# A four-layer graph network on one NeuronCore: 512 of the 2048 columns of an attention step on GpSimd

## The chip, the cores and the metric

The kernel runs on one core of a Trainium2 chip. A core has five engines that run side by side, each through its own queue and in order: TensorE (PE) multiplies matrices into PSUM, VectorE (DVE) and ScalarE (ACT) work element by element and can read PSUM, GpSimd (POOL) works element by element on SBUF, and SyncE (SP) issues the loads. Semaphores order the engines among themselves. The metric is the device time of one execution in microseconds (us), smaller is better. A measurement of this kernel tells a difference of about 0.5%, some 5 us.

## The reference

x has 4096 rows of 64 columns, adj is a 4096 x 4096 matrix of zeros and ones. Four layers follow one another, each x = layernorm(x + layer(x, adj)): a mean over neighbours with a linear map (layer 0), hyperbolic attention (1), a weighted sum in which the weights halve from neighbour to neighbour (2), and hyperbolic attention again (3). The change is in the attention, which layers 1 and 3 share:

```python
x_t = logmap0(x, c)
left = x_t @ w_att[:D, 0]
right = x_t @ w_att[D:, 0]
adj_att = jax.nn.sigmoid(left[:, None] + right[None, :] + b_att[0]) * adj
x_local = logmap(x[:, None, :], x[None, :, :], c)
support_t = jnp.einsum('ij,ijd->id', adj_att, x_local)
return proj(expmap(x, support_t, c), c)
```

For each pair of nodes (i, j) there is one weight: the sigmoid, the edge, and a factor out of logmap (an artanh of the distance over the distance). The sum over j of weight times x_j is a matrix product. So the 16.8 million weights of a layer are the elementwise work, and the rest is small work on rows.

## The kernel before

The 4096 target nodes are cut into four groups of WW = 1024 (GROUPS = 3, 2, 1, 0) and the 4096 source nodes into 32 blocks of 128 (also from the last to the first). attend (L1064) handles one group of one layer. It runs over g = 15 to 0; each g is a pair of blocks, k = 1 and then k = 0, so a layer has 4 x 16 = 64 pairs. In the texts below the pairs of a layer are counted in the order in which they run, from 0 to 63.

For each block of a pair:

- TensorE computes z (128 sources x 1024 targets) in two halves of 512 columns, each from three matmuls: the edges times a constant (L1098), and two products of row data (L1101, L1104). Where there is no edge z is negative.
- ScalarE computes sig, the sigmoid of left plus right (L1113), and sq, the square of a linear function of z (L1116).
- VectorE computes t = max(z, 0) x sig (L1119), with z from PSUM.

After both blocks VectorE does the second pass over the pair, 2048 columns at once: t = (sq + HIGH²) x t (L1121). The product of the two passes is the factor of logmap times the sigmoid. TensorE then adds up t times the source rows xe, in float32, into one PSUM bank for the group (add_up, L1071 to L1082): first k = 1, both halves, then k = 0. This is delayed by two pairs: the list lag holds (g, t), and add_up of a pair is written behind the z products of a later pair.

Buffers: z has three PSUM tiles, sq two tiles of a pair, t three, sig three. So TensorE can be up to three z tiles ahead, and sq of pair g + 2 goes where sq of pair g stood.

The order on TensorE and ScalarE is laid down by the order in which the kernel's text issues work and by dependencies (manual_schedule, FIXED); VectorE's and GpSimd's queues are ordered by the scheduler when the program is built. Between the pairs lies the row work. It is written as generators that tick (L616) advances: every pair ticks at least three times, and each generator says in how many ticks it wants to go on. Three of them matter here:

- norm_rows (L894) and prepare (L914): normalize the rows of a group of nodes and make from them what the next layer's attention needs (hi_lo, lo_hi, src, dst, xe, left, right). Attention can only handle a source block when prepare is done for its group (need, L1086), so the first 16 pairs of a layer run beside this.
- move (L1137): takes the sums of a finished group through expmap, projection and layernorm to the next x. For all groups but the last of a layer it runs on GpSimd (class Small, on_pool), as some ninety operations on 128 x 8 numbers and four on 128 x 512 (L1184, L1265, L1266, L1269), beside the pairs of the following group. VectorE and ScalarE take a part in it: two reductions (L1187, L1189), the first step of each reciprocal square root (L762, three times), a reciprocal (L1233) and a tanh (L1215). Each of these is in the queue of its engine between the operations of the pairs and waits there for GpSimd, and GpSimd waits for it in turn.
- the last group's move runs on VectorE (and in layer 3 it is the end of the kernel).

All loads of adj go through SP's queue, in tiles of 1 MB with six buffers.

Of the kernel before, what the change touches and what calls it, by code (L numbers as in the profile page):

```python
# [15 lines left out]
ALU = mybir.AluOpType  # L16
# [7 lines left out]
W = 512  # L24
# [5 lines left out]
WW = 1024  # L30
# [15 lines left out]
HIGH = 1.3261200051291  # L46
# [14 lines left out]
def gnn_stack_kernel(  # L61
# [15 lines left out]
    nc = tc.nc  # L77
    V = nc.vector
# [492 lines left out]
    def stream(fits):  # L571

        with ExitStack() as st:
# [42 lines left out]
            def tick(n):  # L616
                for _ in range(n):
                    place[1] += 1
                    mark(False)
                    for queue in queues:  # L620
                        while queue and queue[0][1] <= place[1]:
                            wait = next(queue[0][0], None)
                            if wait is None:
                                queue.pop(0)
                                continue
                            queue[0][1] = place[1] + wait
                            if wait:
                                break
                    mark(True)

            def later(steps, second=False, wait=0):
                queues[int(second)].append([steps, place[1] + wait])

            def in_turn(tag, *parts):
                for part in parts:
                    yield from (part or ())
                done.add(tag)
# [5 lines left out]
            def need(tag):  # L643
                while tag not in done:
                    assert any(queues), tag
                    tick(1)
# [53 lines left out]
            def load(s, g):  # L700
                a = loads.tile([P, 2, WW], F32, name="edges")
                nc.sync.dma_start(a, adj[s, :, 2 * g : 2 * g + 2, :])

                return a, a.rearrange("p b i -> p (b i)").bitcast(BF16)[:, 1::2]
# [9 lines left out]
            def nums(name, n=WB):  # L714
                return row.tile([P, n], F32, name=name)
# [320 lines left out]
            def in_order(one, behind):  # L1036

                tc.add_manual_dep(
                    one, behind.name,
                    mybir.DependencyInfo(  # L1040
                        mybir.DependencyClass.NoSync, mybir.DependencyReason.DATA
                    ),
                    reason="order of issue",
                )

            def spread_left(s):

                left_bs[s] = lefts.tile([P, WW], F32, name="left_b")
                for h in range(2):
                    yield from free()  # L1050
                    t = take(F32, P, W)
                    for k in range(SB):
                        nb = s * WB + h * SB + k
                        nc.tensor.transpose(
                            t[:, k * P : (k + 1) * P],
                            left[:, nb : nb + 1].to_broadcast([P, P]),
                            ident,
                        )
                    yield near()
                    nc.scalar.copy(left_bs[s][:, h * W : (h + 1) * W], t)  # L1060
                    held.pop()
                    yield 1

            def attend(layer, s, rate, then):  # L1064

                left_b = left_bs[s]

                acc = ps.tile([P, W], F32, name="acc")
                lag = []

                def add_up(g, t, behind=None):  # L1071

                    for k in (1, 0):
                        j = 2 * g + k
                        for h in range(2):
                            it = nc.tensor.matmul(  # L1076
                                acc[h * D : (h + 1) * D, :], xe[:, j, :],
                                t[:, k, h * W : (h + 1) * W],
                                start=j == BLOCKS[0], stop=j == BLOCKS[-1],
                            )  # L1080
                            if behind is not None:
                                in_order(it.ins, behind.ins)  # L1082

                for g in reversed(range(NB // 2)):
                    _, edge = load(s, g)
                    need((layer, 2 * g // WB))  # L1086
                    if g == 4 and then is not None:
                        later(in_turn((layer, then, "left"), spread_left(then)), True)
                    for k in (1, 0):
                        j = 2 * g + k  # L1090
                        of = slice(j * P, (j + 1) * P)

                        zp = z_tile()
                        for h in range(2):
                            half = zp[:, h * W : (h + 1) * W]
                            to = slice(s * WW + h * W, s * WW + (h + 1) * W)
                            at = k * WW + h * W
                            nc.tensor.matmul(  # L1098
                                half, two_i, edge[:, at : at + W], start=True, stop=False
                            )  # L1100
                            nc.tensor.matmul(  # L1101
                                half, hi_lo[:, of], lo_hi[:, to], start=False, stop=False
                            )
                            last = nc.tensor.matmul(  # L1104
                                half, src[:, of], dst[:, to], start=False, stop=True
                            )
                        if k == 1:
                            if len(lag) == 2:
                                add_up(*lag.pop(0), last)
                            sq = sb.tile([P, 2, WW], F32, name="sq")  # L1110
                            t = sb.tile([P, 2, WW], F32, name="t", bufs=3)
                        sig = sb.tile([P, WW], F32, name="sig", bufs=3)
                        nc.scalar.activation(  # L1113
                            sig, left_b, AF.Sigmoid, bias=right[:, j : j + 1]
                        )
                        nc.scalar.activation(  # L1116
                            sq[:, k], zp, AF.Square, bias=ROOT + OFF, scale=-1.0 / UNIT
                        )
                        V.scalar_tensor_tensor(t[:, k], zp, 0.0, sig, ALU.max, ALU.mult)  # L1119
                        tick(rate)  # L1120
                    V.scalar_tensor_tensor(t, sq, HIGH**2, t, ALU.add, ALU.mult)  # L1121
                    lag.append((g, t))
                    tick(rate)
                for args in lag:
                    add_up(*args)
                sums = row.tile([P, W], F32, name="sums", bufs=2)
                nc.scalar.copy(sums, acc)
                return sums
# [377 lines left out]
            def z_tile():  # L1506
                return ps.tile([P, WW], F32, name="z", bufs=3)

            def attention(layer, curve, rates, behind):

                need((layer, GROUPS[0]))
                for n, s in enumerate(GROUPS):
                    if n:
                        need((layer, s, "left"))
                    anchored[0] = n > 0
                    then = GROUPS[n + 1] if n + 1 < NW else None
                    sums = attend(layer, s, rates[n], then)
                    move_s = in_turn((layer, s, "moved"), move(layer, s, sums, curve))
                    if n:
                        later(  # L1520
                            in_turn((layer + 1, s + 1), there((layer, s + 1, "moved")), behind(s + 1)),
                            True, 9,
                        )
                    apart = 2 if n + 1 == NW and layer == 1 else 0
                    later(move_s, apart)
                    if n + 1 == NW:
                        later(in_turn((layer + 1, s), behind(s)), apart)
                anchored[0] = False
# [174 lines left out]
            t, g = nums("m1", 1), nums("g1", 1)  # L1703
# [4 lines left out]
            sq = row.tile([P, D], F32, name="w_sq")  # L1708
# [21 lines left out]
    with tc.tile_pool(name="fit_ps", bufs=1, space=PSUM) as ps:  # L1730
        t = ps.tile([1, P], F32, name="fit_t")
# [52 lines left out]
```

## Time and profile before

| | |
|---|---|
| three runs | 1073.8, 1074.14, 1077.64 us (median 1074.14) |
| the profiled execution | 1073.46 us |
| its span, first to last instruction | 1071.7 us |
| attention of layer 1, first to last L1121 | 198 to 516 us |
| attention of layer 3, first to last L1121 | 728 to 1039 us |

The span is what the trace shows; the execution has 1.8 us around it. A row of the page's groups reads: line, engine, operation, out<-in with partitions x elements, count, then the busy time of the group in us, the mean duration of one in ns, and the engine's idle time just ahead of it with what ended that. The chain of waits is followed back from the last instruction; its shares say which engine's work lay on the way to the end. Spans on GpSimd include the time in which an operation has started and can't reach its data. The two rows of GpSimd's largest groups in attention, and the row of the tensor engine's accumulation:

```profile
L1076 PE MATMUL acc<-t,xe 128*64 128x512 f32 x1024 | 260.0, 614 | 10.6 <-DVE t L1121 9.7
...
L901 POOL TENSOR_TENSOR sq<-z 128x512 f32<-128x512 f32 x8 | 16.2, 2024 | 168.4 <-DVE z L900 147.3
L1184 POOL TENSOR_TENSOR w_att<-x,u 128x512 f32<-128x512 f32 x6 | 12.7, 2122 | 139.7 <-ACT u L1179 139.7
```

The means of 2024 and 2122 ns hold short and long ones: single operations of this size take from 1.04 to 3.03 us in the trace.

### The profile page before, as it was taken

What the parts mean: (1) busy time and instruction counts of PE and PEld (TensorE: products, weight loads), DVE (VectorE), ACT (ScalarE), POOL (GpSimd) and SP (SyncE); (2) the same over time, 40 slices, a digit from 0 to 9 for tenths busy, and PEclk for the clock granted to TensorE, in tenths of its full rate; (3) what the DMA queues carried; (4) which work ended last, traced back from release to release, by engine and by line L of the source; (5) the groups of instructions that cost most, each with busy time, mean ns of one, the idle gap of its engine ahead of it and who ended that gap; (6) DMA issues with size and microseconds to landing.
All of it is one profiled execution on the core that took longest, in us unless ns stands there. A gap on an engine that the chain in (4) does not pass through costs nothing.

```text
span 1071.7 us, 13656 instructions
## 1 busy us (share of the span) xinstructions
PE 985.7 (92%) x4845; PEld 401.4 (37%) x4845; DVE 919.6 (86%) x1501; ACT 754.4 (70%) x877; POOL 272.3 (25%) x649
## 2 busy tenths in 40 slices
PE   4997998789999999999999989998899999999980
PEld 2454554333333333333333334443333333333320
DVE  7676888999999999999485698829999999999976
ACT  0013122879988889888677778898898888898850
POOL 0011211010044515425500021101102444444162
PEclk9999999989999999999999999999999999999985
DMA  9999999645666656657699979896465666666300
GB/s 340 387 424 356 381 416 377 256 167 197 235 205 227 229 202 210 227 192 240 226 358 324 385 282 342 292 327 223 148 237 194 245 221 209 239 230 229 135 1 24
DMA packets 38580, 271.62 MB, mean 253 GB/s; under 512 B 4710, under 2 KB 4710, under 8 KB 5734
## 3 DMA queue, kind: packets, MB, share of 16 engines
q1 hardware_dynamic: 37728, 270.03, 69.2%
q8 instruction: 40, 0.66, 0.2%
q10 hardware_dynamic: 774, 0.63, 0.2%
q14 instruction: 38, 0.31, 0.1%
HBM read 269.58 MB, written 1.05 MB: 253 GB/s over the span
## 4 chain that ended last, share of the span: by engine, by line
PE 61%; DVE 25%; ACT 6%; DMA 3%; POOL 2%; issue 2%; ACTq 0%; SPq 0%; POOLq 0%; DVEq 0%
PE acc L1076 17%; PE z L1641 9%; PE z L1098 8%; PE z L1104 7%; PE z L1101 7%; DVE t L1119 6%; DVE t L1121 6%; PE acc L1465 4%; DVE junk L844 3%; DMA edges<-in_adj_dram 2%; ACT sq L1648 2%; PE acc L1653 2%; ACT sq L1116 1%; PE z L1653 1%; ACT sig L1113 1%
## 5 line engine op out<-in xcount | busy, mean ns | idle before, releaser
L1119 DVE SCALAR_TENSOR_TENSOR t<-z,sig 128x1024 f32<-128x1024 f32 x256 | 309.8, 1219 | 12.8 <-ACT sq L1116 10.9
L1121 DVE SCALAR_TENSOR_TENSOR t<-sq,t 128x2048 f32<-128x2048 f32 x128 | 295.2, 2307 | 0.2
L1116 ACT ACTIVATE sq<-z 128x1024 f32<-128x1024 f32 x256 | 254.2, 1021 | 56.6 <-PE z L1104 21.6
L1113 ACT ACTIVATE sig<-left_b,right 128x1024 f32<-128x1024 f32 x256 | 286.9, 1149 | 5.3 <-DVE t L1119 4.5
L1076 PE MATMUL acc<-t,xe 128*64 128x512 f32 x1024 | 260.0, 614 | 10.6 <-DVE t L1121 9.7
L1098 PE MATMUL z<-edges,two_i 128*128 128x512 bf16 x512 | 200.9, 392 | 5.5 <-DVE t L1119 5.4
L1104 PE MATMUL z<-dst,src 74*128 74x512 f16 x512 | 194.7, 380 | 0.0
L1101 PE MATMUL z<-lo_hi,hi_lo 128*128 128x512 f16 x512 | 193.8, 378 | 0.0
L1648 ACT ACTIVATE sq<-z 128x512 bf16<-128x512 f32 (+1 forms) x192 | 137.8, 741 | 45.3 <-PE z L1641 44.7
L1076 PEld LDWEIGHTS acc<-t,xe 128*64 128x64 f32 x1024 | 64.3, 137 | 140.5 <-issue 106.0
L1465 PE MATMUL acc<-edges,first 128*128 128x512 bf16 x256 | 80.8, 397 | 17.4 <-DMA edges<-in_adj_dram 17.2
L1098 PEld LDWEIGHTS <-two_i 128*128 128x128 bf16 x512 | 50.3, 98 | 120.5 <-issue 74.5
L1641 PE MATMUL z<-edges,pass_by 128*128 128x512 bf16 x248 | 87.2, 391 | 4.9 <-ACT sq L1648 4.6
L844 DVE SCALAR_TENSOR_TENSOR t<-edges 128x2048 bf16<-128x2048 f32 x32 | 73.0, 2287 | 21.4 <-DMA edges<-in_adj_dram 21.0
L1641 PE MATMUL z<-edges,enter 128*128 128x512 bf16 x256 | 88.8, 389 | 0.0
L844 DVE SCALAR_TENSOR_TENSOR junk<-edges 128x2048 bf16<-128x2048 f32 x32 | 73.1, 2284 | 9.0 <-DMA edges<-in_adj_dram 8.8
L1465 PE MATMUL acc<-edges,third 128*65 128x512 bf16 x256 | 80.4, 396 | 0.0
L1104 PEld LDWEIGHTS <-src 74*128 74x128 f16 x512 | 49.2, 96 | 72.1 <-issue 9.2
L1101 PEld LDWEIGHTS <-hi_lo 128*128 128x128 f16 x512 | 50.2, 98 | 60.6 <-issue 14.6
L901 POOL TENSOR_TENSOR sq<-z 128x512 f32<-128x512 f32 x8 | 16.2, 2024 | 168.4 <-DVE z L900 147.3
L1184 POOL TENSOR_TENSOR w_att<-x,u 128x512 f32<-128x512 f32 x6 | 12.7, 2122 | 139.7 <-ACT u L1179 139.7
L1465 PEld LDWEIGHTS <-first 128*128 128x128 bf16 x256 | 24.3, 98 | 45.1 <-issue 16.2
(402 smaller groups left out, 987.3 us busy)
## 6 DMA issues: line engine op xcount, KB each, us to landing
edges<-in_adj_dram SPq DMA_DIRECT2D x256, 1024.0 KB, 4.9
x<-in_x_dram SPq DMA_DIRECT2D x4, 256.0 KB
out_dram<-x ACTq DMA_DIRECT2D x2, 256.0 KB
out_dram<-x SPq DMA_DIRECT2D x2, 256.0 KB
w_sb<-in_L_gnn_W_dram ACTq DMA_DIRECT2D x1, 32.0 KB, 4.7
w_twice<-in_L_gnn_weight_dram ACTq DMA_DIRECT2D x2, 16.0 KB, 8.7
given<-in_L_gnn_b_dram ACTq DMA_DIRECT2D x1, 0.2 KB
given<-in_L_gnn_bias_dram ACTq DMA_DIRECT2D x1, 0.2 KB
```

The source lines that it names most:

```text
L844: V.scalar_tensor_tensor(junk, a, 0.0, a, ALU.not_equal, ALU.not_equal, accum_out=odd[:, n : n + 1])
L1076: it = nc.tensor.matmul(acc[h * D : (h + 1) * D, :], xe[:, j, :], t[:, k, h * W : (h + 1) * W], start=j == BLOCKS[0], stop=j == BLOCKS[-1],)
L1098: nc.tensor.matmul(half, two_i, edge[:, at : at + W], start=True, stop=False)
L1101: nc.tensor.matmul(half, hi_lo[:, of], lo_hi[:, to], start=False, stop=False)
L1104: last = nc.tensor.matmul(half, src[:, of], dst[:, to], start=False, stop=True)
L1113: nc.scalar.activation(sig, left_b, AF.Sigmoid, bias=right[:, j : j + 1])
L1116: nc.scalar.activation(sq[:, k], zp, AF.Square, bias=ROOT + OFF, scale=-1.0 / UNIT)
L1119: V.scalar_tensor_tensor(t[:, k], zp, 0.0, sig, ALU.max, ALU.mult)
L1121: V.scalar_tensor_tensor(t, sq, HIGH**2, t, ALU.add, ALU.mult)
L1465: nc.tensor.matmul(accs[h][:m], lhs[:, j, :], edge[:, at : at + W], start=j == BLOCKS[0], stop=j == BLOCKS[-1],)
L1641: nc.tensor.matmul(z[:, h : h + W], lhs, rhs[:, h : h + W], start=j == BLOCKS[0], stop=True, skip_group_check=True,)
L1648: weighed[0] = nc.scalar.activation(w, z[:, :n], AF.Exp, bias=-(OFF_EDGE + CUT) * LN2, scale=-LN2)
```

## The change

The second pass over a pair is split. t and sq are seen as flat rows of 2048 columns. VectorE handles columns 0 to 1535 (all of k = 0 and the first half of k = 1) as before. The last 512 columns (the second half of k = 1) go to GpSimd, [...]it does an addition in place in sq and then a product into t.

```diff
@@ -1118,7 +1118,16 @@
                         )
                         V.scalar_tensor_tensor(t[:, k], zp, 0.0, sig, ALU.max, ALU.mult)
                         tick(rate)
-                    V.scalar_tensor_tensor(t, sq, HIGH**2, t, ALU.add, ALU.mult)
+                    flat_sq, flat_t = (o.rearrange("p k i -> p (k i)") for o in (sq, t))
+                    mine, its = slice(0, 2 * WW - W), slice(2 * WW - W, 2 * WW)
+                    V.scalar_tensor_tensor(
+                        flat_t[:, mine], flat_sq[:, mine], HIGH**2, flat_t[:, mine],
+                        ALU.add, ALU.mult,
+                    )
+                    nc.gpsimd.tensor_scalar(
+                        flat_sq[:, its], flat_sq[:, its], HIGH**2, None, ALU.add
+                    )
+                    nc.gpsimd.tensor_mul(flat_t[:, its], flat_t[:, its], flat_sq[:, its])
                     lag.append((g, t))
                     tick(rate)
                 for args in lag:
```

Everything else is the same text. As VectorE's and GpSimd's queues are ordered when the program is built, the neighbours of these operations in the queues can differ from before.

## The prediction

> **What bounds the kernel now.** First the page's table of engines and its chain of waits, then the groups, then the timeline of a quiet stretch. One *pair* g means two source blocks (k=1, then k=0); a layer has 64 pairs, and m(g) and S(g) below are the VectorE steps L1119 and L1121 of pair g.
>
> ```profile
> span 1071.7 us, 13656 instructions
> PE   985.7 (92%) x4845; PEld 401.4 (37%) x4845; DVE 919.6 (86%) x1501; ACT 754.4 (70%) x877; POOL 272.3 (25%) x649
> ...
> PE 61%; DVE 25%; ACT 6%; DMA 3%; POOL 2%; issue 2%; ACTq 0%; SPq 0%; POOLq 0%; DVEq 0%
> ...
> L1119 DVE SCALAR_TENSOR_TENSOR t<-z,sig 128x1024 f32<-128x1024 f32 x256 | 309.8, 1219 | 12.8 <-ACT sq L1116 10.9
> L1121 DVE SCALAR_TENSOR_TENSOR t<-sq,t 128x2048 f32<-128x2048 f32 x128 | 295.2, 2307 | 0.2
> ```
>
> The page makes TensorE the bound and VectorE the second. That is an average; what the change is worth is read in attention. A row of the timeline is start, duration, engine, operation:
>
> ```profile
> 427.63 2.28 DVE L1121 SCALAR_TENSOR_TENSOR t<-sq,t 128x2048 f32<-128x2048 f32 x1
> 429.84 2.50 DVE L1119 SCALAR_TENSOR_TENSOR t<-z,sig 128x1024 f32<-128x1024 f32 x2
> 432.25 2.28 DVE L1121 SCALAR_TENSOR_TENSOR t<-sq,t 128x2048 f32<-128x2048 f32 x1
> ...
> 431.01 1.94 PE L1076 MATMUL acc<-t,xe 128*64 128x512 f32 x8
> ...
> 435.62 0.65 PE L1076 MATMUL acc<-t,xe 128*64 128x512 f32 x2
> ```
>
> VectorE goes from S to S in 4.62 us without idling; its own work is about 4.57 (2.20 for S start to next start, 2.4 for two m). TensorE goes from one accumulation to the next in 4.61: eight L1076 take 1.87 until the next z product starts, twelve z products of about 0.22 and a gap of 0.09 make up 2.74. In most pairs of 246 to 512 us and 787 to 1030 us the spacing is exactly 4.62. So both engines stand at the limit; with VectorE relieved, TensorE's 4.62 remains.
>
> The third resource is the access to SBUF that VectorE shares with GpSimd:
>
> ```profile
> 334.81 0.20 POOL L1246 TENSOR_TENSOR w<-w,mt 128x8 f32<-128x8 f32 x1
> 334.98 0.23 POOL L750 TENSOR_SCALAR pool_t<-px 128x8 f32<-128x8 f32 x1
> 335.17 2.35 POOL L1247 TENSOR_SCALAR mt<-w 128x8 f32<-128x8 f32 x1
> ...
> 363.83 3.15 DVE L1121 SCALAR_TENSOR_TENSOR t<-sq,t 128x2048 f32<-128x2048 f32 x1
> ...
> 363.79 1.04 POOL L1266 TENSOR_TENSOR u<-u,q 128x512 f32<-128x512 f32 x1
> 364.91 3.12 POOL L1269 TENSOR_TENSOR x<-u,w_att 128x512 f32<-128x512 f32 x1
> 373.28 1.16 POOL L1304 TENSOR_TENSOR x_hl<-x,x_hl 128x512 f16<-128x512 f32 x1 [5.25 <-ACT x_hl L1303]
> ```
>
> L1247 has eight columns and takes 2.35 us because S runs from 335.15 to 337.43. At 363.83 it is the other way: L1266 is under way, S takes 3.15 instead of 2.28, and then L1269 stands still until S ends.[...]
>
> [...]S (sq and t, both SBUF) blocks as above, while m (z in PSUM, sig in SBUF) is 1172 to 1225 ns in all 256 cases.[...] The trace has 1.04 us for a product of 512 columns against 0.20 for 8: 1.67 ns[...] per column, so the measurement is used for the product. A GpSimd addition of 512 columns isn't in the trace.
>
> **The change part by part.**
>
> 1. *S shrinks from 2048 to 1536 columns.* [...]0.53 less in each of 128 pairs, 68 us of VectorE. Almost all of it lies beside TensorE's 4.62. It reaches the end only where VectorE alone is late:
>  - Start of each attention: accumulations 0 to 7 of layer 1 lie at 200.54 to 246.36, 45.8 us for 7 x 4.62 = 32.3; layer 3 has 56.9 for 46.2 at its start. Most of the excess is the burst of row operations between two S (25 operations ahead of S(5)), which stays. I count four S per layer: 4 x 0.53 x 2 = 4.2 us.
>  - The last S of each layer: 0.53 x 2 = 1.1 us.
>  - Quiet stretches: from 246 us to the end layer 1 takes 10.7 us more than 56 x 4.62, some 8 of it TensorE's own row products. Of the rest I count 1 us a layer, 2.
>  Together 7 us; ends 3 and 11.
>
> 2. *GpSimd gets an addition A(g) and a product T(g) in each pair.* T: 1.045 us free of S. A: its small form L750 takes 0.24; [...]I take 0.70, ends 0.55 and 0.95. They take the last 512 columns of k=1, so A needs the first sq and T the first m of the pair. A and T can run under both m, where nothing contends, but not under S.
>
> 3. *What that does to GpSimd's queue.* GpSimd runs in order, and the row work of the previous group (move) passes through it: in layer 1 from 310.1 to 402.2 us, then 493.9; the repeat is 90 to 92 us, 19 pairs. Its shared access in such a repeat:
>  - S: 19 x 1.67 (1.75, plus 0.06 to restart, less 0.14 of a blocked operation's own start that is hidden) = 31.7
>  - T: 19 x (1.045 + 0.06) = 21.0; A: 19 x (0.70 + 0.06) = 14.4
>  - 90 small row operations, added from the stretches without S (11 in 2.86 us, 31 in 7.9, 13 in 2.4, 21 in 5.4, 14 in 3.7): 22.2; four or five of 512 columns: 4.8
>  Sum 94.1 us for 91 us of time. It was 22.2 + 4.8 + 19 x 2.2 = 69. So the access goes from three quarters to over full. Beyond the 3 us, GpSimd must at times wait for VectorE or ScalarE (d, r_t2, th, den, twice n); I estimate 1.5 us per repeat that can't be caught up. Per repeat 4.5 us late.
>
> 4. *Who waits for it.* TensorE's accumulation of g now waits for T(g), for its very first matmuls (k=1). From the end of m(g) of k=1 to that accumulation there are two periods less sq and m: 9.24 - 2.3 = 6.9 us, or 8.2 where both z blocks of g+2 stand ahead. In the built queues fewer do: in layer 1 the accumulation stands ahead of the second z block in 35 of 62 pairs, 12 before. ScalarE's sq of g+2 overwrites what A and T read (two buffers), about 6.9 us too. In GpSimd's built queue T(22) stands behind 17 row operations and A(22), T(32) behind 14 small and 3 large. By hand T(22) ends 6.7 us after its m, T(32) about 9. Behind A and T in turn stand the row operations for which VectorE (L762, L1233) and ScalarE (tanh, L1215) wait in the midst of the pairs. Tanh has no slack: L1209 ends at 316.40, L1215 starts at 316.44. The other row steps had 4 to 9 us. So lateness is free until about 3 us a layer, then it stops the pairs.
>  Two and a half repeats a layer: 2.5 x 4.5 - 3 = 8 us, 16 in both layers.
>
> 5. *The other side of the access.* S waits when T or A is under way, at most 1.05, by their share about 0.25 on average. VectorE: 2 x 1.17 + 1.75 + 0.25 = 4.3 a pair, under 4.62, so nothing. If A were 0.95 it would still be under. The order of loads on SP is the same in the built program; ScalarE's work (about 4.3 a pair) is the same. At the end of layer 1 the built queue of VectorE has the wait for den two pairs earlier than before; I leave up to 3 us for it in the range.
>
> Sum: 16 - 7 = +9 us. The profiled execution took 1073.46 (span 1071.7 and 1.8 around it), 0.7 under the median 1074.14; so about 1083 us.
>
> **Rivals.**
> - *GpSimd keeps up* (faster). If A is 0.55 and the lateness never exceeds the 6.9 us, only part 1 counts: 1074 - 7 = 1067, 1063 with the larger end. For it: GpSimd is busy for only 25% on the page. Against it: the 94 of 91 above, and tanh without slack.
> - *A wash.* With A at 0.55 the sum is 91 of 91 us, and only the waits cost: 2.5 x 1.5 x 2 = 8, against 7: 1075, within 1072 to 1078. For it: both sums are small and of opposite sign. Against it: it needs the lowest price of A.
> - *GpSimd becomes the bound outright* (slower still). A at 0.95: 19 x 0.25 = 4.8 more a repeat, 9.3 late: (2.5 x 9.3 - 3) x 2 = 40, less 7: 1107.[...]
> - That S doesn't get shorter (the flattened form costs what it did) would give 1090 and is unlikely[...].
>
> **How the numbers follow.** Forecast (slower by 4 to 18 us) 0.37, 1083, own range 1078 to 1092. Keeps up 0.20. A wash 0.20. GpSimd as the bound 0.23. A measurement of this kernel tells 0.5%, 5.4 us: 1068.8 and 1079.5 are the limits. Faster 0.20 (all of the first rival); same 0.24 (the wash and the forecast's lower end); slower 0.56. The range of 8 in 10 takes in most of both outer cases: 1063 to 1108.
>
> **What would show it.** S at 1.75 us; A at 0.7 and T at 1.05 where no S lies over them, else up to 2.8. GpSimd's busy time 272 + 128 x 1.75 = 496 us and more by blocked time. New idle time of TensorE ahead of L1076 put down to GpSimd, and of ScalarE ahead of sq, mostly after L767's chains. VectorE with idle time ahead of L1119. If the accumulations keep 4.62 throughout, part 4 is wrong and the first rival holds; if the quiet pairs without row work are longer than 4.62 too, the price of A or of the shared access is wrong.

## The result and the profile after

The changed kernel takes 1171.49 us (median of four runs, 1167.3 to 1173.61) against 1073.97 (1072.89 to 1077.64) for the kernel before: a ratio of 1.0888, 95% interval 1.0855 to 1.0922. It is 97.5 us slower; the forecast was +9.

The page after, in the order in which the page before was read: span and engines, GpSimd's busy share in 40 equal slices of the span (in tenths), the chain of waits, the groups. As in the prediction, m and S are VectorE's first and second pass, A and T GpSimd's addition and product.

```profile
span 1171.9 us, 14081 instructions
PE 1039.8 (89%) x4845; PEld 411.9 (35%) x4845; DVE 894.1 (76%) x1501; ACT 761.2 (65%) x877; POOL 688.0 (59%) x905
...
POOL 0011122766999998979600021046679998999893
...
PE 48%; DVE 23%; POOL 15%; ACT 7%; issue 3%; DMA 3%; ACTq 0%; SPq 0%; POOLq 0%; DVEq 0%
...
L1119 DVE SCALAR_TENSOR_TENSOR t<-z,sig 128x1024 f32<-128x1024 f32 x256 | 308.1, 1218 | 119.4 <-ACT sq L1116 117.7
...
L1127 POOL TENSOR_SCALAR sq<-sq 128x512 f32<-128x512 f32 x128 | 242.5, 1895 | 88.4 <-ACT sq L1116 85.0
L1123 DVE SCALAR_TENSOR_TENSOR t<-sq,t 128x1536 f32<-128x1536 f32 x128 | 240.4, 1878 | 1.5
L1130 POOL TENSOR_TENSOR t<-t,sq 128x512 f32<-128x512 f32 x128 | 192.4, 1503 | 33.6 <-DVE t L1119 8.0
```

VectorE is only 25.5 us less busy (919.6 to 894.1) and now idles 119.4 us ahead of m (12.8 before). GpSimd went from 272 to 688 us, where the prediction had said 496 and more. POOL rose from 2% to 15% of the chain. At 59% GpSimd doesn't look full, but 59% is again a mean over stages: from 293 to 557 us and from 879 to 1142 us the slices stand at 7 to 9 tenths.

The views of the lines of A, T and S give minimum, median and maximum in ns:

```profile
L1127 POOL TENSOR_SCALAR sq<-sq x128: 1480/1492/3025, 195.9 to 1138.3; 128x512 f32<-128x512 f32 x128
```
```profile
L1130 POOL TENSOR_TENSOR t<-t,sq x128: 1258/1278/2794, 198.6 to 1139.9; 128x512 f32<-128x512 f32 x128
```
```profile
L1123 DVE SCALAR_TENSOR_TENSOR t<-sq,t x128: 1706/1757/2807, 202.4 to 1139.0; 128x1536 f32<-128x1536 f32 x128
```

Minimum and median lie close together, so the median is the price without waiting. A costs 1.49 us, not 0.70, and T 1.28, not 1.045. S is what was forecast, 1757 ns in the median.

Who waits for it, in the view of waits (total us, times, longest):

```profile
DVE t L1119 <- ACT sq L1116: 117.7, 96, 4.8
...
ACT sq L1116 <- PE z L1104: 63.6, 65, 4.0
PEld acc L1076 <- POOL t L1130: 59.6, 27, 5.9
...
PE acc L1076 <- POOL t L1130: 37.4, 15, 5.0
...
ACT sq L1116 <- POOL t L1130: 31.4, 19, 5.2
...
DVE den L1242 <- POOL den L1239: 18.2, 2, 9.3
```

These are the two waits that the prediction's part 4 named, TensorE's accumulation and ScalarE's sq of the pair after next. The weight load (PEld) and the matmul (PE) can stand in the same wait (at 548.61 us both start, after 3.41 and 2.53 us of waiting for one T), so their two sums aren't added. VectorE's wait for sq follows from both: ScalarE's sq waits for T and, for 63.6 us, for TensorE's z. Not all of it is a loss: where GpSimd has nothing to do in the pairs (e14 below), VectorE waits 66.0 us for sq, and the kernel takes no longer than the one before. The last line is the wait for den at the end of an attention. The timeline shows its place (start, duration; in brackets the idle time and who ended it):

```profile
544.37 1.49 POOL L1127 TENSOR_SCALAR sq<-sq 128x512 f32<-128x512 f32 x1
544.40 1.23 DVE L1119 SCALAR_TENSOR_TENSOR t<-z,sig 128x1024 f32<-128x1024 f32 x1 [0.18 <-ACT sq L1116]
...
547.29 1.26 POOL L1130 TENSOR_TENSOR t<-t,sq 128x512 f32<-128x512 f32 x1
548.59 1.02 ACT L1116 ACTIVATE sq<-z 128x1024 f32<-128x1024 f32 x1 [0.59 <-POOL t L1130]
...
548.61 3.61 PE L1076 MATMUL acc<-t,xe 128*64 128x512 f32 x6 [2.53 <-POOL t L1130]
548.64 1.49 POOL L1127 TENSOR_SCALAR sq<-sq 128x512 f32<-128x512 f32 x1
...
550.22 1.26 POOL L1130 TENSOR_TENSOR t<-t,sq 128x512 f32<-128x512 f32 x1
...
554.30 0.24 POOL L1239 TENSOR_SCALAR den<-den 128x8 f32<-128x8 f32 x1
554.57 0.20 DVE L1242 RECIPROCAL den<-den 128x8 f32<-128x8 f32 x1 [8.94 <-POOL den L1239]
554.69 1.71 DVE L1123 SCALAR_TENSOR_TENSOR t<-sq,t 128x1536 f32<-128x1536 f32 x1
```

From 544.4 to 554.5 GpSimd works through A, five row operations, T, A, T and fourteen row operations. TensorE and ScalarE both start when the first T ends (548.55), and VectorE stands idle for 8.94 us, the next S in its queue behind the reciprocal, until GpSimd has come to den.

Where the time was lost can be read from the pairs. For each run, the start of the first m of pair g less its start in the kernel before, both counted from pair 0 of the layer, gives how late pair g is (us, layer 1; worked out from the starts of VectorE's first step; the experiments are told of below):

```
pair                       0      8     19     31     42     47     61     63
after                    0.0   -0.7    1.5   12.5   17.4   28.6   38.6   46.7
no addition (e1)         0.0   -1.7   -0.3    3.6    4.9    8.6   12.6   15.4
short addition (e2)      0.0   -1.5    0.1    5.7    8.2   12.2   16.8   21.1
rows on VectorE (e3)     0.0   -1.2    0.1    8.2   13.4   15.4   26.5   28.1
first group only (e4)    0.0    0.2    3.0    2.5    2.5    2.5    2.5    2.5
den later (e9)           0.0   -0.9    1.2    8.2   24.4   31.6   40.1   40.2
short rows (e10)         0.0   -0.4    1.8    7.1   11.2   15.8   21.9   26.9
e1 with short rows (e13) 0.0   -1.1    0.3    2.8    3.2    6.3    8.4   10.3
shorter S alone (e14)    0.0   -7.0   -6.2   -4.3   -4.6   -1.2   -1.1    0.0
```

Against the kernel before, the changed kernel loses almost nothing up to pair 19, where GpSimd has little row work, and 45 us from there to the end of the layer. Layer 3 loses 50.2 in the same places.

### The profile page after: what moved, and what is told of

Read it like the earlier page. It is cut to its first block, busy times and chain, and to the rows that moved or that the text cites. A ratio compares the mean times of both kernels' runs of the same rounds, so it can differ in the third digit from the quotient of the medians.

```text
span 1171.9 us, 14081 instructions
## 1 busy us (share of the span) xinstructions
PE 1039.8 (89%) x4845; PEld 411.9 (35%) x4845; DVE 894.1 (76%) x1501; ACT 761.2 (65%) x877; POOL 688.0 (59%) x905
## 3 DMA queue, kind: packets, MB, share of 16 engines
q1 hardware_dynamic: 37728, 270.03, 63.6%
## 4 chain that ended last, share of the span: by engine, by line
PE 48%; DVE 23%; POOL 15%; ACT 7%; issue 3%; DMA 3%; ACTq 0%; SPq 0%; POOLq 0%; DVEq 0%
PE acc L1076 14%; PE z L1650 8%; DVE t L1119 6%; PE z L1098 5%; PE z L1104 5%; PE z L1101 5%; POOL sq L1127 4%; DVE t L1123 4%; POOL t L1130 3%; PE acc L1474 3%; ACT sq L1116 3%; DVE junk L844 2%; DMA edges<-in_adj_dram 2%; ACT sig L1113 2%; ACT sq L1657 1%
## 5 line engine op out<-in xcount | busy, mean ns | idle before, releaser
L1119 DVE SCALAR_TENSOR_TENSOR t<-z,sig 128x1024 f32<-128x1024 f32 x256 | 308.1, 1218 | 119.4 <-ACT sq L1116 117.7
L1076 PE MATMUL acc<-t,xe 128*64 128x512 f32 x1024 | 305.5, 637 | 54.3 <-POOL t L1130 37.4
L1116 ACT ACTIVATE sq<-z 128x1024 f32<-128x1024 f32 x256 | 259.2, 1020 | 116.0 <-PE z L1104 63.6
L1127 POOL TENSOR_SCALAR sq<-sq 128x512 f32<-128x512 f32 x128 | 242.5, 1895 | 88.4 <-ACT sq L1116 85.0
L1123 DVE SCALAR_TENSOR_TENSOR t<-sq,t 128x1536 f32<-128x1536 f32 x128 | 240.4, 1878 | 1.5
L1130 POOL TENSOR_TENSOR t<-t,sq 128x512 f32<-128x512 f32 x128 | 192.4, 1503 | 33.6 <-DVE t L1119 8.0
L1076 PEld LDWEIGHTS acc<-t,xe 128*64 128x64 f32 x1024 | 72.7, 141 | 213.2 <-issue 106.1
L901 POOL TENSOR_TENSOR sq<-z 128x512 f32<-128x512 f32 x8 | 14.9, 1862 | 111.2 <-DVE z L900 101.4
L1444 POOL TENSOR_TENSOR sq<-z 128x512 f32<-128x512 f32 x4 | 6.1, 1532 | 119.4 <-DVE z L1442 83.2
```

The source lines that it names most:

```text
L1076: it = nc.tensor.matmul(acc[h * D : (h + 1) * D, :], xe[:, j, :], t[:, k, h * W : (h + 1) * W], start=j == BLOCKS[0], stop=j == BLOCKS[-1],)
L1116: nc.scalar.activation(sq[:, k], zp, AF.Square, bias=ROOT + OFF, scale=-1.0 / UNIT)
L1123: V.scalar_tensor_tensor(flat_t[:, mine], flat_sq[:, mine], HIGH**2, flat_t[:, mine], ALU.add, ALU.mult,)
L1127: nc.gpsimd.tensor_scalar(flat_sq[:, its], flat_sq[:, its], HIGH**2, None, ALU.add)
L1130: nc.gpsimd.tensor_mul(flat_t[:, its], flat_t[:, its], flat_sq[:, its])
```

## The experiments

Three theories stood against each other. (1) GpSimd and the access it shares with VectorE are over-full: the prediction's part 3, with the measured prices, asks for 31.7 + 25.5 + 29.5 + 27 = 113.7 of 91 us. (2) Order: T stands behind row operations, whatever they cost, and the buffers leave too little slack. (3) A, T and S block each other in every pair. "Shared access" stands for what the traces show of it: an A that starts under an S takes up to 3.03 us instead of 1.49, a T up to 2.79 instead of 1.28, an S behind a T up to 2.81 instead of 1.76, while m stays at 1196 to 1226 ns in all 256 cases after, 241 of them beside work of GpSimd. That the two meet at SBUF is the author's reading. Ratios are to the kernel before, run beside each, with 95% intervals.

### A left out, A at the forecast price, half the columns

```diff
 e1: the addition left out
-                    nc.gpsimd.tensor_scalar(
-                        flat_sq[:, its], flat_sq[:, its], HIGH**2, None, ALU.add
-                    )
 e2: the addition on 186 columns
+                    few = slice(2 * WW - 186, 2 * WW)
                     nc.gpsimd.tensor_scalar(
-                        flat_sq[:, its], flat_sq[:, its], HIGH**2, None, ALU.add
+                        flat_sq[:, few], flat_sq[:, few], HIGH**2, None, ALU.add
 e12: 256 columns on GpSimd
-                    mine, its = slice(0, 2 * WW - W), slice(2 * WW - W, 2 * WW)
+                    mine, its = slice(0, 2 * WW - W // 2), slice(2 * WW - W // 2, 2 * WW)
```

> GpSimd's addition A is left out, its product T stays (so the constant HIGH² is missing in 512 of 2048 columns). Theory 1, the access that VectorE and GpSimd share is over-full: with the durations of the changed kernel's trace a repeat of 19 pairs needs S 31.7 + T 19 x 1.34 = 25.5 + A 19 x 1.55 = 29.5 + rows 27 = 113.7 of 91 us; without A it needs 84, so the time goes back to 1065 to 1080 us. Theory 2, GpSimd's order: T stands behind the row operations whatever it costs, and the buffers give too little slack; then T is still late and the time stays at 1110 us or more. Theory 3, the mutual blocking with S in every pair: about half of the loss stays, 1110 to 1130 us.

Measured: 1102.87 us, 1.0264 (1.0216 to 1.0311). That is none of the three: it lies between 1080, where theory 1 ends, and 1110, where the other two begin.

> A on 186 columns instead of 512 (the constant is missing in 326 columns), so that it costs 0.237 + 178 x 2.49 ns = 0.68 us, what the prediction took for it. Theory 1: 31.7 + 25.5 + 14.1 + 27 = 98.3 of 91, 7.3 us late per repeat, (2.5 x 7.3 - 3) x 2 - 7 = 24, so 1098 us (1085 to 1110). Theory 2 (order and slack): 1140 or more, as A and T keep their places in the queue. A loss in proportion to A's duration without any threshold gives 1171 - 97 x 0.81 / 1.49 = 1118.

Measured: 1117.69 us, 1.0372 (1.0334 to 1.0410), with A at 686 ns in the median. This is the price that the prediction took, and the loss is 42 us, not 24. The proportional rule hits 1118 by accident: by the same rule e1 should have lost nothing.

> The same change with 256 columns on GpSimd instead of 512. A 0.237 + 248 x 2.49 ns = 0.85, T 0.73, S 2.01 us: 36.7 + 17.4 + 15.0 + 27 = 96.1 of 91 us, 5.1 late per repeat; on the scale of the runs so far (84 of 91: 1103, 98.3: 1118, 113.7: 1171) some 1115. A loss in proportion to the columns gives 1122. If a smaller share is free, 1070 to 1080.

Measured: 1114.40 us, 1.0363 (1.0336 to 1.0390), as read off the scale. Together: T alone costs 28 us, A's first 0.69 us another 15, and its remaining 0.81 us 55. A is the largest part, 70 of 97; it is not the whole.

### Cheaper addition, fewer row operations

```diff
 e7: an addition of two inputs
+    high2 = const.tile([P, 1], F32, name="high2")
+    V.memset(high2, HIGH**2)
...
-                    nc.gpsimd.tensor_scalar(
-                        flat_sq[:, its], flat_sq[:, its], HIGH**2, None, ALU.add
+                    nc.gpsimd.tensor_add(
+                        flat_sq[:, its], flat_sq[:, its], high2.to_broadcast([P, W])
                     )
 e10, e11, e13: one refining step (on the kernel after, before, and e1)
-                    for _ in range(3):
+                    for _ in range(1 if self.on_pool else 3):
```

> The changed kernel with its addition written as an addition of two tensors, the second one column repeated. If a two-input operation of this size costs 1.28 us as T does, A gets 0.21 us cheaper, 19 x 0.21 = 4 us per repeat, and the time falls by about 5 x 4 = 20 us to some 1152 (1140 to 1160). If GpSimd's price is the same for every operation of this size, or the repeated column costs more, 1165 or more.

Measured: 1147.55 us, 1.0671 (1.0635 to 1.0707). This addition takes 1040 ns, less than T, so it saves 0.45 a pair rather than 0.21 and 24 us in all; S rose from 1878 to 2026 ns in the mean, which took part of it back (the last section says why).

> The changed kernel with one step instead of three in each reciprocal square root on GpSimd (the two refining steps are left out there): 24 small operations fewer per move, at 0.28 us each 6.7 us. If GpSimd is over-full, every us of row work counts: five repeats x 6.7 = 33 us less, 1138 (1125 to 1150). If the loss is A, T and S in the pairs alone, or the waits at fixed places, 1160 or more.

> The kernel before with the same 24 operations left out, the control: GpSimd has room there (69 of 91 us), so 1070 to 1077. If it gains 20 us or more here too, the row operations counted before the change already, and the run above tells nothing.

Measured: 1145.73 us, 1.0657 (1.0626 to 1.0687), 26 us less than the changed kernel; in the kernel before the same omission gives 2 us, 0.9973 (0.9957 to 0.9989). The 144 small operations left out in the two layers are 40 us at 0.28 each; hidden before, they hold up the end by some 24 us after. That fits theory 1, with not the whole of each operation counting. Theory 2 would gain as well, with fewer operations ahead of T; the runs with more slack below speak on it.

### The rows taken off GpSimd

```diff
-                    eng = nc.gpsimd if on_pool else V
+                    eng = V
...
-                    nc.gpsimd.tensor_scalar(t, in0, scalar, None, op0)
-                    nc.gpsimd.tensor_tensor(out, t, in1, op1)
+                    V.tensor_scalar(t, in0, scalar, None, op0)
+                    V.tensor_tensor(out, t, in1, op1)
...
-                E = V if last else nc.gpsimd
+                E = V
```

> The changed kernel with the row work of move on VectorE instead of GpSimd, so GpSimd has only A and T in the pairs. Theory 1: the shared access is asked for 31.7 + 25.5 + 29.5 = 87 of 91 us; VectorE has 19 x (2.4 + 1.75) = 79 plus some 10 us of row work, just under the limit, so 1075 to 1100 us. Theory 2: T has no row operations ahead of it any more, also 1070 to 1100. Theory 3, that A, T and S block each other in every pair: unchanged, 1130 us or more.

Measured: 1135.92 us, 1.0559 (1.0526 to 1.0591): what theory 3 expected, but not for its reason. The page's engines, then the waits:

```profile
PE 998.1 (88%) x4759; PEld 403.2 (36%) x4845; DVE 1001.7 (88%) x2065; ACT 760.5 (67%) x877; POOL 507.0 (45%) x341
```
```profile
PEld acc L1076 <- DVE t L1123: 81.3, 84, 3.3
...
PE acc L1076 <- DVE t L1123: 39.4, 54, 3.0
...
DVE t L1119 <- ACT sq L1116: 9.1, 15, 2.6
```

TensorE now waits for S, and VectorE for sq for 9.1 us instead of 117.7: with the rows gone TensorE and ScalarE hardly wait for T any more (weight load 0.7 us, sq 1.1). But 564 more operations cost VectorE 107.6 us, 0.19 each and 18 per move where 10 had been estimated, and VectorE became the bound. The total tells nothing between the theories. The waits speak against 3 as far as it makes T late; S was still held up in some pairs (mean 1818 ns, median 1746).

### The split where there are no rows

```diff
-                    flat_sq, flat_t = (o.rearrange("p k i -> p (k i)") for o in (sq, t))
+                    if s != GROUPS[0]:
+                        V.scalar_tensor_tensor(t, sq, HIGH**2, t, ALU.add, ALU.mult)
+                    else:
+                        flat_sq, flat_t = (o.rearrange("p k i -> p (k i)") for o in (sq, t))
...
```

> The split only in the first group of each layer, pairs 0 to 15, where GpSimd has hardly any row work; the other three groups as before the change. Theories 1 and 2: A + T + S = 1.49 + 1.28 + 1.75 = 4.52 of 4.62 us a pair fits, so 1070 to 1078 us. Theory 3: each pair loses by the blocking, a quarter of the 97 us, 1090 to 1100. If the prediction's part 1 is right (a shorter S at the start of a layer), up to 4 us are gained: 1070.

Measured: 1081.22 us, 1.0059 (1.0044 to 1.0074). A quarter of the split costs 6 us, not 24, so blocking in every pair alike is not the cause; there is no gain either. The table has it 3 us late at pair 19, in both layers. The section on e14 sets it against a shorter S alone.

### More slack

```diff
-            loads = pool("f_loads", 6)
+            loads = pool("f_loads", 4)
...
-                            if len(lag) == 2:
+                            if len(lag) == 3:
...
-                            sq = sb.tile([P, 2, WW], F32, name="sq")
-                            t = sb.tile([P, 2, WW], F32, name="t", bufs=3)
+                            sq = sb.tile([P, 2, WW], F32, name="sq", bufs=3)
+                            t = sb.tile([P, 2, WW], F32, name="t", bufs=4)
```

e5 is this on e1, e6 on the changed kernel, e8 only its first edit on the kernel before.

> The addition left out (the constant is missing in 512 of 2048 columns) and a pair more of slack: accumulation three pairs behind instead of two, four tiles of t, three of sq, paid for with four tiles of edges instead of six. Without the slack this lost 28 us while the account of the shared access is not full (84 of 91 us), and its trace shows one hole of 4 to 5 us per repeat where T stands behind some 24 row operations. If that loss is order and slack, it goes: not over 1082 us, less what four tiles of edges cost in the kernel before. If it is a loss in the steady pairs (blocking of S), it stays at 1095 to 1105.

> The changed kernel with the same added slack. If the addition's part of the loss (1171 against 1103) is throughput, 113.7 of 91 us asked of the shared access, slack helps once per stretch and not in each repeat: 1125 to 1160. If it is order as well, the time goes to 1075 to 1100.

> The kernel before with four tiles of edges instead of six, the control for the two runs with more slack. In attention a tile is asked for every 4.62 us, so nothing is lost there; in layer 0 and the weighted sum the tiles come faster, 0 to 15 us: 1075 to 1090.

Measured: e8 1109.61 us, 1.0311 (1.0279 to 1.0343). Four tiles of edges cost 35 us, far more than expected, all ahead of pair 0 of the two layers (25.8 us by layer 1, 36.7 by layer 3; inside the attentions -1.0 and 0.0). Against that control e5 (1128.88; 1.0467, 1.0412 to 1.0522) loses 19.3 where e1 lost 27.6, and e6 (1195.61; 1.1107, 1.1063 to 1.1151) loses 86.0 where the change lost 97. So a pair more of slack is worth 8 and 11 us by the totals, the first no more than the error of the three runs behind it, and some 4 and 6 by the starts of the pairs: theory 2, as a matter of slack, isn't the main cause. With the control's 35 us, e5's expectations become at most 1117 for order and slack and 1130 to 1140 for a loss in the steady pairs; 1128.88 lies at the second.

### The wait for den moved

```diff
-                    yield G.wait(14)
+                    yield G.wait(14) + 4
```

> The changed kernel with the reciprocal of den asked for four ticks later, so that in VectorE's queue it stands behind the last pair of each attention (before the change it stood there) instead of two pairs ahead of it. In the trace of the changed kernel VectorE waits 18.2 us at this reciprocal, in two places. If that wait is a loss of its own, 12 to 20 us come back: 1151 to 1160. If the pairs behind it are late for GpSimd in any case, 1167 to 1175.

Measured: 1198.22 us, 1.1147 (1.1120 to 1.1175), 27 us worse, outside both expectations. The wait did shrink:

```profile
DVE den L1242 <- POOL den L1239: 5.5, 2, 2.9
```

and the last pair of layer 1 is 40.2 us late instead of 46.7. But the row work behind the reciprocal moved too: the last GpSimd move of layer 1 ends at 608 instead of 580 us, the stretch from the first m of the last pair of layer 1 to the first m of layer 3 grew from 217.2 to 240.3, and that from the first m of the last pair of layer 3 to the end of the span from 38.1 to 48.3. The wait was where the late row work came due; put elsewhere, it comes due in the next stage.

### What T and the shorter S cost by themselves

e13 is the refining step's edit on e1; e14 leaves T out of e1 as well, so that GpSimd has no work in the pairs:

```diff
-                    nc.gpsimd.tensor_mul(flat_t[:, its], flat_t[:, its], flat_sq[:, its])
```

> The addition left out and one step instead of three in each reciprocal square root on GpSimd. The product alone lost 28 us though the account of the shared access is at 84 of 91. If that loss comes from T standing behind runs of row operations and row steps of VectorE standing behind T, fewer of them make it smaller: 1080 to 1095. If it is a loss in each pair (T and S blocking each other, 128 x 0.2), it stays at 1098 to 1105.

> VectorE's second pass on 1536 columns and nothing on GpSimd (for the last 512 columns the factor of the second pass is left out): the relief of VectorE alone. The prediction's part 1 gives 7 us, ends 3 and 11: 1067 (1063 to 1071). If TensorE's 4.62 us and the row work of the start leave nothing to gain: 1073 to 1076.

Measured: e13 1096.47 us, 1.0205 (1.0172 to 1.0237); e14 1071.71 us, 0.9973 (0.9954 to 0.9992). e13 takes 6 of the 28 us away, 2 of which the kernel before gains too; its interval lies across both expectations, and 6 us is about the error of the two runs. In the starts of the pairs it is 5.1 us in layer 1 and 6.1 in layer 3, so row operations seem to carry part of what T costs in the attentions.

In the table T (e1 less e14, layer 1) costs 5.3 us by pair 8, where GpSimd has little row work but VectorE has that of prepare, 0.6 from there to pair 19, and 9.5 more to the end, over half of it in the last 16 pairs. The split in the first group alone (e4 less e14) has the same shape: 7.2 us by pair 8 of layer 1 and 0.3 from there to pair 15; in layer 3 6.8 and 0.9. So e4's 6 us hide a gain that A and T ate up at the start of each layer.

The traces show a way in which T does this. With the same 1501 operations VectorE is busy for 34 us more, the time in which an operation stands still included; e1, then e14:

```profile
PE 993.5 (90%) x4759; PEld 402.5 (37%) x4845; DVE 892.4 (81%) x1501; ACT 759.1 (69%) x877; POOL 471.9 (43%) x777
```
```profile
PE 987.1 (92%) x4759; PEld 404.2 (38%) x4845; DVE 858.1 (80%) x1501; ACT 756.8 (71%) x877; POOL 233.4 (22%) x649
```

S makes 13 of the 34 us (241.2 against 228.0); the rest is in VectorE's row operations. An example is L762, the first step of a reciprocal square root, in the kernel before and in e1:

```profile
L762 DVE TENSOR_SCALAR r_t<-t x8: 163/165/172, 309.8 to 1050.5; 128x8 int32<-128x8 int32 x8
```
```profile
L762 DVE TENSOR_SCALAR r_t<-t x8: 160/1240/1245, 310.0 to 1077.4; 128x8 int32<-128x8 int32 x8
```

The timeline of e1, in which T is L1127:

```profile
308.37 1.75 DVE L1123 SCALAR_TENSOR_TENSOR t<-sq,t 128x1536 f32<-128x1536 f32 x1
...
308.53 2.72 POOL L1127 TENSOR_TENSOR t<-t,sq 128x512 f32<-128x512 f32 x1 [1.33 <-DVE t L1119]
...
310.03 1.24 DVE L762 TENSOR_SCALAR r_t<-t 128x8 int32<-128x8 int32 x1
...
311.19 1.21 DVE L1119 SCALAR_TENSOR_TENSOR t<-z,sig 128x1024 f32<-128x1024 f32 x1
```

T starts under S, stands still until S ends at 310.12, and runs to 311.25. L762, behind S in VectorE's queue, then stands still until T ends, and m starts only after that. Nine of the 24 L762 in e1 start under T and take 1.16 to 1.25 us, each to 25 to 29 ns after T's end. TensorE's accumulation in e1 then waits for S much more than for T:

```profile
PE acc L1076 <- DVE t L1123: 18.5, 27, 1.9
...
PE acc L1076 <- POOL t L1127: 2.7, 3, 1.2
```

In e14 it waits 4.8 us for S. So what T costs by itself reaches the end at least in part by way of VectorE, that is by the blocking of theory 3, and hardly by T being late. How much of the 28 us this makes wasn't tried.

e14 is the whole benefit that the change could have: 3.5 us (interval 0.9 to 5). Layer 1 gains 6 to 7 us by pair 19, layer 3 5.4, nearly all given back by pair 63. Why it is given back wasn't tried.

## Why the prediction was wrong

The step that failed is part 2's price: "I take 0.70, ends 0.55 and 0.95" for A. It is 1.49 us. The small form's 0.24 was right; the slope was not: 0.686, 0.851 and 1.492 us for 186, 256 and 512 columns make 2.5 ns a column, where 0.70 for 512 columns and 0.24 for 8 mean 0.9 (0.6 and 1.4 at the ends). No row of the trace before has this form at 512 columns: 0.70 was the author's estimate, which no trace had shown. T's 1.045 was the second error of the same kind: L1266, from which it came (1044 ns in the median), has an operand of eight numbers repeated over 64 columns. L1184 and L1269 of the kernel before read two full tiles, have minima of 1187 and 1185 ns, and were the nearer rows; T itself is 1278.

That step isn't the whole. Of the 88 us between the forecast's +9 and the 97 measured, 55 are A above 0.69 us. With A at the forecast price (e2) the loss is still 42 us, and with T alone (e1) 28. The second step that failed is part 5's "under 4.62, so nothing": its 4.3 us hold only S and m, and T makes VectorE busy for 34 us more (e1 against e14), and TensorE's accumulation waits for S.

Point by point:

1. S at 1.75 us: right. The medians are 2281 ns for 2048 columns before and 1757 for 1536 after, so 0.52 less where 0.53 was forecast; the two make 1.02 ns a column. The 7 us of gain: 3.5 in e14. The gain at the starts was there (4.2 counted, more found) but wasn't kept.
2. Prices: as above. Both ends for A lay below the truth.
3. The account: the 0.14 us of hidden start stand in the trace before, where GpSimd's products of eight columns, 0.20 us alone, end 0.06 after the S that held them up; the 0.06 to restart was the author's estimate. With the two prices corrected it asks for 113.7 of 91 us instead of 94.1. Continued by the prediction's own rule, with its 1.5 us of waits a repeat, that is (2.5 x 24.2 - 3) x 2 - 7 = +108, without them +100, against 97.5 measured. That fit is partly luck, because of point 4. That GpSimd's row work counts is shown by e10 and e11.
4. Who waits: the accumulation, sq and den, as named. That lateness is free until about 3 us a layer wasn't tried by itself. But the account of point 3 gives +31 for e2 and about -6 for e1, and they lost 42 and 28. In e1 that isn't T being late, for which TensorE hardly waits: the account of lateness has no place for what point 5 left out. Den, for which up to 3 us had been left in the range, shows as 18.2 us of waiting; e9 says that it isn't a loss of its own.
5. S waiting for T or A, estimated 0.25: its mean is 0.12 over its median and 0.17 over its minimum. The size was about right; that it comes to nothing was not, as e1 and e14 show, and VectorE's row operations, which wait for T too, were left out.

Of the rivals, "GpSimd becomes the bound outright" named the mechanism, priced with A at 0.95. "GpSimd keeps up" leaned on the 25% of the page; it would have needed a split without rows beside it, and even there e4 gains nothing. No run of a complete computation beat the kernel before. The wide end of 1108 failed with A's upper bound: an operation that the trace didn't show was bounded by estimates alone, while nothing excluded that it cost more than the product beside it.

## What to carry to other kernels

Before work is moved to an engine that looks idle, add up its new work and its old in the stage where they meet, per repeat, with the price of the very instruction form; if no row of the trace has that form, keep the upper bound wide, and take for a two-input operation a row with two full operands. Here work on an access that two engines share cost time well before the access was full: 28 us at 84 of 91 us by the account (e1). So ask of the relieved engine too which of its operations, the small ones included, will stand behind the moved ones. And ask first what the relieved engine can give: VectorE was 86% busy, yet a quarter less second pass for nothing was worth 3.5 us, as TensorE stands at the same 4.62 us.

## What the runs showed of the hardware

GpSimd's addition of a constant (one input, 512 columns, float32) takes 1.49 us, its addition of two inputs with one column repeated 1.04; the view of e7:

```profile
L1129 POOL TENSOR_TENSOR sq<-sq,high x128: 1027/1040/2604, 195.9 to 1109.4; 128x512 f32<-128x512 f32 x128
```

The operation with fewer inputs is the dearer one, by 43%.

T and A hold the shared access differently. In the prediction's two examples (L1247 behind S, S behind L1266) the later operation stands still until the earlier one ends. T agrees; A, when it is the earlier one, doesn't. The timeline after:

```profile
296.04 1.28 POOL L1130 TENSOR_TENSOR t<-t,sq 128x512 f32<-128x512 f32 x1
296.21 2.73 DVE L1123 SCALAR_TENSOR_TENSOR t<-sq,t 128x1536 f32<-128x1536 f32 x1
...
297.28 3.01 POOL L1127 TENSOR_SCALAR sq<-sq 128x512 f32<-128x512 f32 x1
```
```profile
240.00 1.50 POOL L1127 TENSOR_SCALAR sq<-sq 128x512 f32<-128x512 f32 x1 [1.10 <-ACT sq L1116]
...
240.56 1.75 DVE L1123 SCALAR_TENSOR_TENSOR t<-sq,t 128x1536 f32<-128x1536 f32 x1
```

In the first, S ends 1.61 us after T does; in the twelve longest S under such an overlap it is 1.612 to 1.617. Then A stands still until S is over; the 39 A that start under an S end 1.35 to 1.36 us after it. In the second A is under way, and S takes its usual 1.75, as in all 29 cases in which A has at most 0.95 us still to run (1.742 to 1.759). Only where A still has 1.26 to 1.47 us to run (nine times) is S longer, 1.99 to 2.20, and then it ends 0.73 after A: by these numbers A lets S in an estimated 0.88 us before its own end (1.61 less 0.73). The two-input addition of e7 holds S to its end again (1.61 to 1.62 us), which is why S got longer there.

A VectorE operation with a single SBUF input can wait as well. L762 has one input and in e1 stands still until T ends (1.24 us instead of 0.17). The reciprocal of den has one too, and it takes 0.19 us, not held up, in the same place of e1, behind S with T waiting (T from 332.55 to 335.28, S to 334.14):

```profile
334.06 0.19 DVE L1239 RECIPROCAL den<-den 128x8 f32<-128x8 f32 x1
```

What makes the two differ, the traces don't show.
